# A three-layer graph kernel: heavier split rows, fewer two-sided tiles, and elementwise work moved to ScalarE and GpSimd

## The chip, the cores and the metric

One core of a Trainium2 chip. The metric is the device time of one execution in microseconds, as the median of several runs.

## The reference

The graph has N = 6250 nodes with 128 features and E = 200000 edges. The edges are sorted by destination, and destinations are drawn as 6250·u², so low-numbered nodes have hundreds to thousands of incoming edges and high-numbered ones a few dozen. The input is layer-normalised and clipped at zero. Then come three layers of the same form:

```
agg = segment_max(h[src], dst)           # per node: elementwise max over its sources' rows; 0 without edges
h   = leaky_relu(agg @ Wl + bl + h @ Wr, 0.01)
```

The widths are 128 → 256 → 256 → 128, and the output is x + h. Nearly all the work is in `segment_max`: 200000 rows of 128 or 256 floats, three times.

## The kernel before

**Tiles and planes.** Nodes are cut into 50 tiles of 127 (R = 127), sources into 25 pairs of tiles. For a tile of destinations and a source pair, TensorE multiplies the pair's rows (kept as two fp32r halves, whose sum is exact) with a one-hot matrix: each of the 128 columns picks one source row, so one product fetches one edge per destination. DVE then takes the maximum of the product in PSUM and the running result `acc` (`maxima`, line 1026). The one-hot matrix `hot` is made by ScalarE from a byte index (lines 983 and 985).

A *narrow* tile ("n") has one column set per pair: both source tiles are multiplied into the same PSUM tile, and one maximum takes it. A *middle* ("m"), *wide* ("w") or *extra* ("x") tile has one column set for each of the two source tiles, so each is multiplied and taken by itself: the same matmuls, two maxima. The nodes of the first three tiles (VT = 3) have too many edges; they are split into *virtual* rows of up to CUT_V edges in NV tiles of 128, which count as wide, with a second plane "x" each. A scan joins their parts later (`Joined`).

**Groups and steps.** The tiles form five groups: 24 narrow; the middle ones; the NV virtual with their extras; 8 wide; 4 narrow. For every group and pair there are *parts* of up to 8 tiles, which share one `hot` for each source tile. A part is cut into *steps* of 512 columns by two feature halves (layers 1 and 2) or of 1024 columns (layer 0). `parts_in` sorts the parts of a pair, and the steps follow part by part. Layer 0 has 225 steps, layers 1 and 2 have 375 each.

**Lists.** An edge that found no plane (its destination has another edge with a source in the same tile or pair) goes to a list. The lists are sorted by length, and CAPS says how many entries each block of 128 of them has. For each entry GpSimd issues one indirect DMA that gathers 128 rows from the table (`Listed.gather`, line 1064), followed by a memset of 300 elements that serves nothing but as a pause (line 1068). DVE takes the maxima of the gathered rows. There are 506 gathers in a layer. They need the whole table of the layer.

**Nodes.** When a tile's planes and lists are done, `Node` fetches its list result, merges it (DVE), multiplies by the weights (PE, line 1147 and 1149), copies the sum out of PSUM (ScalarE, 1151), applies the leaky relu (DVE, 1158 or 1162), and, for the next layer, transposes the rows and splits them into halves (`halves`; `keep_halves`, DVE, line 918).

**Making the indices.** In layer 0 the kernel still sorts the edges out. `flag_rows` finds edges that must go to lists, `pick_rows` and `rank_rows` build the lists, and `expand` finds for every pair and row the edge of that pair: each row entry holds a source number in which the tile takes the high bits, an exclusive-or with the wanted tile's number leaves a number below 128 where it fits (DVE, line 772, five pairs in five instructions), and a tree of minima finds it (778, 779). `lookups` turns that into the byte index. These pieces are *chores* that are spread over steps 0 to 150 of layer 0.

**Order.** The order of each engine's instructions is written out by hand. An agenda gives each piece a step and a rank in it (LET, TURN, MAXIMA, ROWS, REST, LINEAR, MERGE, SOONER, GATHER, FETCH). Gathers are spread evenly over a layer's steps (wide steps count 1.25), and their maxima come 6 steps later (4 at the least in layer 0). A node's `rows` comes a step after its `linear`, ahead of that step's gathers.

Of the kernel before, what the change touches and what calls it, by code (L numbers as in the profile page):

```python
# [32 lines left out]
F32 = mybir.dt.float32  # L33
# [10 lines left out]
P = 128  # L44
BIG = 2.0**127
EPS = 1e-5
SLOPE = 0.01
# [8 lines left out]
VT, NV, CUT_V = 3, 6, 96  # L56
CAPS = (
    (13, 11, 10, 9, 8, 8, 7, 7, 6, 6, 6, 6, 5, 5, 5, 4, 4, 4, 3, 3, 3, 2, 2, 1),
    (26, 22, 18, 13, 9, 5),
    (14, 11, 10, 8, 7, 7, 6, 5, 4, 4, 3),  # L60
    (33, 24, 20, 17, 15, 13, 11, 9),
    (14, 10, 8, 6),
# [5 lines left out]
HOT, HOTS = 1024, 6  # L68
# [3 lines left out]
PAUSE = 300  # L72


@with_exitstack
def kernel(ctx: ExitStack, tc: tile.TileContext, x, src, dst,
# [16 lines left out]
    PAST = NG << 8  # L93
    assert NT * P <= PAST and PAST + NT * P < LEAF
# [3 lines left out]
    NARROW = list(range(26, NT)) + list(range(22, 26))  # L98
    MIDDLE = list(range(11, 22))
# [4 lines left out]
        [("m", i) for i in range(NM)],  # L104
# [5 lines left out]
    PLANES = [units + (EXTRA[4:] + EXTRA[:4] if k == VIRT else []) for k, units in enumerate(GROUPS)]  # L110
# [165 lines left out]
    nc.vector.scalar_tensor_tensor(scol, c_i, 1.0, srci, op0=OP.add, op1=OP.add)  # L276
# [255 lines left out]
    def flag_rows(us, S):  # L532
# [6 lines left out]
        if wide:  # L539
            ri, g, o, seen = (S(i, I32, n, J) for i in (0, 1, 2, 1))  # L540
            nc.vector.tensor_copy(ri, r[:, :, :J])
            nc.vector.tensor_scalar(g, ri, 8, None, op0=OP.arith_shift_right)
            nc.vector.tensor_tensor(b, one[:, None, :].to_broadcast([P, n, J]), g, op=OP.logical_shift_left)
            nc.vector.tensor_scalar(o, ri, 24, 31, op0=OP.logical_shift_left, op1=OP.arith_shift_right)
# [33 lines left out]
    def pick_rows(k, i0, us, S):  # L578
# [12 lines left out]
        nc.vector.tensor_scalar(picked[k][:, i0 : i0 + n, :], top, -float(LEAF), 0.0, op0=OP.add, op1=OP.max)  # L591
# [174 lines left out]
    def expand(us, J, g0, s, least, S):  # L766
# [3 lines left out]
        t = S(0, I16, BATCH * n, J).rearrange("p (i u) j -> p i u j", i=BATCH)  # L770
# [12 lines left out]
    turns = itertools.cycle(("tr", "z"))  # L783
    stored = [0] * len(GROUPS)

    def lookups(us, least, s, pool, tags=("v", "v8")):

        n = len(us)
        wide = us[0][0] != "n"
        v = pool.tile([P, n, NG], BF16, tag=tags[0], name="v", bufs=1 + (tags[0] == "v"))  # L790
# [3 lines left out]
        while i < n:  # L794
# [4 lines left out]
            if us[i] in EXTRA:  # L799
                m = min(m, 4 - us[i][1] % 4)  # L800
# [85 lines left out]
    for g0 in range(0, NG, BATCH):  # L886
        expand(L0, CB, g0, 0, least, S_first)
# [27 lines left out]

    def keep_halves(layer, a, h, pr):
# [46 lines left out]
    hots, live, done_with = {}, [0], [0, 0]  # L963
# [12 lines left out]
    def one_hot(layer, k, g, c, w, odd, s):  # L976
# [4 lines left out]
        hot = work.tile([P, HOT], F32R, tag="hot", name="hot", bufs=HOTS)  # L981
# [4 lines left out]
        hots[layer, k, g, c, s] = hot  # L986
        live[0] += 1

    def products(step, s, p):
# [5 lines left out]
        hot = hots[layer, k, g, c0, s]  # L995
# [10 lines left out]
        if c * P + w == c0 * P + pw:  # L1006
            del hots[layer, k, g, c0, s]
            done_with[-1] += 1
# [20 lines left out]
    class Listed:  # L1029
# [25 lines left out]
        def gather(self, t):  # L1055
# [12 lines left out]
            nc.gpsimd.memset(gap_t, 0.0)  # L1068
# [31 lines left out]
    class Node:  # L1100
# [9 lines left out]
        def fetch(self):  # L1110
# [12 lines left out]
            if layer == 2:  # L1123
                n = min(R, N - a * R)
                self.xt = later.tile([P, D], F32, tag="xt", name="xt", bufs=4)
# [16 lines left out]
        def linear(self):  # L1142
# [163 lines left out]
    for s in range(2):  # L1306
        late_lookups(GROUPS[1], s)
# [467 lines left out]
```

## Time and profile before

| | |
|---|---|
| median of 3 runs | 3166.22 us (3161.16 to 3170.59) |
| profiled execution | 3162.05 us, span 3160.2 us |
| PE, DVE, ACT, POOL busy | 2332.1, 2717.8, 1433.9, 2430.8 us |
| gathers of the lists (POOL) | 1518, 1523.9 us, and as many pauses, 566.5 us |

The engines are PE (TensorE's matmuls), PEld (its weight loads), DVE (VectorE), ACT (ScalarE) and POOL (GpSimd). They work side by side; busy time on one hides behind another unless something waits for it. The times of stretches below count from the span's start: the setup lasts to 229 us; layer 0's steps run to 1216 us, layer 1's to 2201 us and layer 2's to about 3130 us. In layer 1 the gathers start in earnest at about 1264 us, and the first nodes are merged at about 1850 us; in layer 2 the two times are about 2260 and 2835 us.

### The profile page before, as it was taken

To read this page: it belongs to the slowest core of one execution; us is meant where nothing else is said; L and a number is where in the kernel's file an instruction comes from. 1 tells how busy PE (TensorE), PEld (TensorE's weight loads), DVE (VectorE), ACT (ScalarE), POOL (GpSimd) and SP (SyncE) were. 2 spreads that over 40 slices of the span, in tenths; PEclk is the share of its full clock that TensorE was granted. 3 is DMA by queue.
4 is the path that set the end of the run, shared out by engine and by line. 5 is a ranking of instruction groups with operands and counts; after the bars stand their busy time and mean duration, and the time that the engine had idled before them with its cause. 6 is when DMAs were issued, how large, how long until landed. Compare 5 with 4: busy or idle time off the path is not lost.

```text
span 3160.2 us, 37328 instructions
## 1 busy us (share of the span) xinstructions
PE 2332.1 (74%) x9394; PEld 1710.8 (54%) x9394; DVE 2717.8 (86%) x4441; ACT 1433.9 (45%) x2394; POOL 2430.8 (77%) x3424
## 2 busy tenths in 40 slices
PE   1024554456566778899888878889999988888997
PEld 1023333334344455677666656666676666666665
DVE  6668988987898975999999988876799999998995
ACT  5214443333544666555454434444555545443342
POOL 6666888688778883888888786763688888788882
PEclk9996766777767999999999999999999999999998
DMA  9322334266645797556454456778455554555675
GB/s 259 116 65 82 116 111 115 80 179 215 197 156 174 221 270 243 160 157 189 144 153 151 149 162 217 235 217 265 155 172 162 174 141 156 157 153 174 201 221 153
DMA packets 303458, 538.58 MB, mean 170 GB/s; under 512 B 57245, under 2 KB 165589, under 8 KB 302595
## 3 DMA queue, kind: packets, MB, share of 16 engines
q1 hardware_dynamic: 206573, 302.97, 29.7%
q0 software_dynamic: 78592, 196.07, 23.0%
q10 hardware_dynamic: 18070, 37.07, 3.1%
q8 instruction: 79, 1.29, 0.2%
q14 instruction: 144, 1.18, 0.1%
HBM read 409.84 MB, written 126.04 MB: 170 GB/s over the span
## 4 chain that ended last, share of the span: by engine, by line
DVE 19%; PE 16%; POOL 12%; DMA 6%; issue 6%; ACT 1%; SPq 0%; DVEq 0%; POOLq 0%; ACTq 0%
DVE acc L1026 13%; PE pg L1002 11%; POOL g L1064 8%; DMA g<-table,let 4%; POOL gap_t L1068 3%; DVE g L1079 2%; DVE g L1084 2%; PE z_p L1147 2%; PE z_p L1149 1%; DMA out_dram<-s 1%; DMA pair_sb<-pair 1%; ACT hot L985 0%; DMA agg_v<-best,end_i 0%; PE hT_p L908 0%; DMA xt<-in_x_dram 0%
## 5 line engine op out<-in xcount | busy, mean ns | idle before, releaser
L1002 PE MATMUL pg<-hot,pair_sb 128*128 128x512 f32 (+1 forms) x7500 | 2036.3, 421 | 414.2 <-DVE acc L1026 241.3
L1002 PEld LDWEIGHTS pg<-hot,pair_sb 128*128 128x128 f32 x7500 | 1436.1, 202 | 873.4 <-issue 285.9
L1064 POOL DMA_INDIRECT g<-table,let x1518 | 1523.9, 1004 | 492.6 <-issue 237.6
L1026 DVE TENSOR_TENSOR acc<-acc,pg 128x1024 f32<-128x1024 f32 (+4 forms) x1614 | 1663.6, 1057 | 207.1 <-PE pg L1002 164.7
L985 ACT ACTIVATE hot<-idx_sb 128x1024 fp32r<-128x1024 uint8 (+2 forms) x1050 | 909.6, 886 | 714.0 <-PE pg L1002 548.5
L1068 POOL MEMSET gap_t<- 128x300 f32 x1518 | 566.5, 373 | 0.7
L983 ACT ACTIVATE hot<-idx_sb,last_b 128x1024 fp32r<-128x1024 int8 (+1 forms) x300 | 310.3, 1034 | 37.2 <-PE pg L1002 24.9
L1118 POOL DMA_INDIRECT agg<-best,end_i x141 | 140.1, 994 | 104.1 <-PE aT_p L1134 60.5
L1151 ACT COPY s<-z_p 127x256 f32<-127x256 f32 (+1 forms) x150 | 50.4, 336 | 363.2 <-PE z_p L1149 325.8
L1079 DVE TENSOR_TENSOR g<-g 128x1024 f32<-128x1024 f32 (+6 forms) x214 | 207.8, 971 | 0.3
L1084 DVE TENSOR_TENSOR g<-g 128x256 f32<-128x256 f32 (+3 forms) x377 | 183.2, 487 | 11.2 <-issue 0.2
L1147 PE MATMUL z_p<-wr,hT_in 128*128 128x256 f32 (+1 forms) x500 | 138.7, 395 | 0.6 <-DMA hT_in<-across 0.6
L1149 PE MATMUL z_p<-wl,mz 128*128 128x256 f32 (+1 forms) x500 | 121.4, 360 | 11.9 <-DVE mz L1140 11.9
L908 PE MATMUL hT_p<-ident,h 128*128 128x128 f32 x200 | 44.3, 306 | 88.2 <-DVE h L1158 82.0
L973 DVE TENSOR_SCALAR idx_sb<-idx_sb,own_b 128x512 int32<-128x512 int32 (+3 forms) x125 | 73.4, 588 | 35.8 <-DMA idx_sb<-idx 30.6
L910 ACT COPY hT<-hT_p 128x254 f32<-128x254 f32 x100 | 37.1, 371 | 145.8 <-PE hT_p L908 129.0
L1149 PEld LDWEIGHTS z_p<-wl,mz 128*128 128x128 f32 x500 | 89.5, 204 | 25.1 <-DVE mz L1140 14.9
L652 POOL DMA_INDIRECT picks<-picked,to_i x53 | 61.5, 1161 | 48.2 <-DVE rank_f L629 23.5
L1140 DVE TENSOR_TENSOR mz<-acc,aT_p 128x256 f32<-128x256 f32 (+1 forms) x141 | 52.4, 371 | 53.3 <-PE aT_p L1134 53.3
L1147 PEld LDWEIGHTS z_p<-wr,hT_in 128*128 128x128 f32 x500 | 80.7, 203 | 31.7 <-issue 13.3
L908 PEld LDWEIGHTS hT_p<-ident,h 128*128 128x128 f32 x200 | 24.1, 149 | 120.1 <-issue 54.9
L806 ACT CAST v<-lk_p 25x1024 uint8<-25x1024 bf16 (+4 forms) x16 | 11.5, 747 | 165.7 <-PE lk_p L804 165.7
(291 smaller groups left out, 1298.0 us busy)
## 6 DMA issues: line engine op xcount, KB each, us to landing
pair_sb<-pair SPq DMA_DIRECT2D x106, 512.0 KB
idx_sb<-far SPq DMA_DIRECT2D x100, 384.0 KB
pair<-pr SPq DMA_DIRECT2D x100, 256.0 KB
g<-table,let POOLq DMA_INDIRECT x1518
pair_sb<-pair SPq DMA_DIRECT2D x85, 256.0 KB
idx_sb<-idx SPq DMA_DIRECT2D x50, 384.0 KB
far<-idx_sb ACTq DMA_DIRECT2D x50, 384.0 KB
idx_sb<-far SPq DMA_DIRECT2D x50, 352.0 KB
```

The costliest lines, as they stand in the source:

```text
L973: nc.vector.tensor_scalar(words, words, own_b.bitcast(I32)[:, 0:1], None, op0=OP.bitwise_xor)
L983: nc.scalar.activation(hot[:, :w], far_b.bitcast(I8), AF.Relu, bias=last_b, scale=-1.0)
L985: nc.scalar.activation(hot[:, :w], far_b, AF.Relu, bias=1.0, scale=-1.0)
L1002: nc.tensor.matmul(to, pr[:, s, i, kk * P : (kk + 1) * P], hot[:, o : o + bw], start=((alone or s == 0) and i == 0), stop=((alone or s == ...
L1026: nc.vector.tensor_max(to, to, of)
L1064: nc.gpsimd.indirect_dma_start(out=self.tiles[q, b][:, i, :], out_offset=None, in_=tables[self.layer], in_offset=bass.IndirectOffsetOnAxis ...
L1068: nc.gpsimd.memset(gap_t, 0.0)
L1079: nc.vector.tensor_max(base[:, : i + 1, :], base[:, : i + 1, :], g[:, : i + 1, :])
L1084: nc.vector.tensor_max(base[:, :h, :], base[:, :h, :], base[:, w - h : w, :])
L1118: nc.gpsimd.indirect_dma_start(out=self.agg[:, : self.F], out_offset=None, in_=of, in_offset=bass.IndirectOffsetOnAxis(ap=at, axis=0),)
L1147: nc.tensor.matmul(z_p, self.hT[:, i, :], wr[layer][:, i, :], start=False, stop=False)
L1149: nc.tensor.matmul(z_p, self.m[:, i, :], wl[layer][:, i, :], start=False, stop=(i == K - 1))
```

## The change

- **Distances.** Source numbers are stored with a stride of 256 instead of 128 (FAR). For wide, middle, extra and virtual rows, `expand` computes |source − 256·tile| with a ScalarE activation (Abs, the bias from a table `keys`) in place of the DVE's exclusive-or. It is issued one chore ahead of the tree that uses it, in one of four areas of scratch. Narrow rows keep the exclusive-or, and get two more DVE operations in `lookups`; `pick_rows` gets two more.
- **Relu.** ScalarE writes relu(z) and relu(−0.01·z), and GpSimd subtracts the two (`in_place`). The subtraction in `keep_halves` moves to GpSimd too. Each such operation cancels the next two pauses of the gathers (SPARE = 2; cancelled pauses are carried over when no gather follows).
- **Tiles.** NV 6 → 5 with CUT_V 96 → 104. Tiles 19 to 21 leave the middle for the narrow kind, in the same group (8 middle and 3 narrow). CAPS are new: 503 gathers a layer instead of 506.
- **Steps.** `parts_in` merges single steps of the groups, with at most two parts open at once (OPEN = 2). In layer 0 each part is one step.
- **Buffers.** Layers 1 and 2 get two more `hot` buffers (MORE = 2), and `xt` gets 8 instead of 4.

```diff
-VT, NV, CUT_V = 3, 6, 96
+VT, NV, CUT_V = 3, 5, 104
...
-    NARROW = list(range(26, NT)) + list(range(22, 26))
-    MIDDLE = list(range(11, 22))
+    NARROW = list(range(26, NT)) + list(range(22, 26)) + list(range(19, 22))
+    MIDDLE = list(range(11, 19))
...
-        [("m", i) for i in range(NM)],
+        [("m", i) for i in range(NM)] + [("n", i) for i in range(28, NN)],
...
         for i in range(BATCH):
-            nc.vector.tensor_scalar(
-                t[:, i, :, :], r[:, :, :J], ((g0 + i) << 8) | (s << 7), None, op0=OP.bitwise_xor
-            )
+            a = 2 * (g0 + i) + s
+            if wide:
+                nc.scalar.activation(t[:, i, :, :], r[:, :, :J], AF.Abs, bias=keys[:, a : a + 1], scale=1.0)
+            else:
+                nc.vector.tensor_scalar(t[:, i, :, :], r[:, :, :J], a * FAR, None, op0=OP.bitwise_xor)
...
+    def in_place(out, a, b):
+        nc.gpsimd.tensor_tensor(out, a, b, op=OP.subtract)
+        paused[0] += SPARE
+
     def keep_halves(layer, a, h, pr):
         F = widths[layer]
-        nc.vector.tensor_sub(pr[:, 1, :F], h[:, :F], pr[:, 0, :F].bitcast(F32))
+        in_place(pr[:, 1, :F], h[:, :F], pr[:, 0, :F].bitcast(F32))
...
-            nc.gpsimd.memset(gap_t, 0.0)
+            if paused[0]:
+                paused[0] -= 1
+            else:
+                nc.gpsimd.memset(gap_t, 0.0)
...
-            nc.scalar.copy(s[:R, :FO], z_p[:R, :])
+            self.h = b = h_ts[turn_h[0] % len(h_ts)]
+            turn_h[0] += 1
+            nc.scalar.activation(s[:R, :FO], z_p[:R, :], AF.Relu)
+            nc.scalar.activation(b[:R, :FO], z_p[:R, :], AF.Relu, scale=-SLOPE)
...
-                nc.vector.scalar_tensor_tensor(h[:R, :FO], s[:R, :FO], SLOPE, s[:R, :FO], op0=OP.mult, op1=OP.max)
+                in_place(h[:R, :FO], s[:R, :FO], h[:R, :FO])
...
+        open_, steps = set(), []
+        while any(rows):
+            now = sorted(r[0][:2] + (r,) for r in rows if r)
+            r = next((r for _, k, r in now if k in open_ or len(open_) < OPEN), None)
+            _, k, part, c, last = r.pop(0)
+            open_.add(k)
+            if last:
+                open_.remove(k)
+            steps.append((k, part, c))
+        return steps
```

## Rows read from the trace of the kernel before

**Rows 1.** Busy time by stretch: start:end, length, then each engine's busy us (instructions).
```profile
229.00:545.00 316.00, 160.85 (x516) 119.09 (x516) 284.38 (x655) 138.24 (x191) 259.18 (x376) 0.71 0.38 113
545.00:1216.00 671.00, 427.56 (x1421) 286.40 (x1421) 573.18 (x1166) 318.77 (x568) 529.42 (x743) 0.78 0.62 187
1264.00:1850.00 586.00, 525.43 (x2132) 391.60 (x2131) 556.60 (x596) 299.41 (x435) 510.32 (x748) 0.98 0.51 157
1850.00:2201.00 351.00, 302.29 (x1342) 227.42 (x1341) 276.86 (x355) 142.59 (x298) 225.90 (x306) 0.97 0.71 223
2260.00:2835.00 575.00, 513.85 (x2082) 379.83 (x2081) 546.29 (x587) 290.25 (x420) 496.83 (x730) 0.99 0.52 157
2835.00:3160.00 325.00, 269.61 (x1324) 206.60 (x1322) 271.79 (x378) 109.91 (x218) 225.07 (x304) 0.93 0.63 189
```

**Rows 2.** Waits of DVE, 1264 to 1850 us: total us, times, longest.
```profile
DVE acc L1026 <- PE pg L1002: 12.8, 21, 1.9
```

**Rows 3.** One line of instructions: POOL's gathers, 1264 to 1850 us.
```profile
L1064 POOL DMA_INDIRECT g<-table,let x373: 946/952/2002, 1264.4 to 1849.2; - x187
...
  issue: 55.8, 322
```

**Rows 4.** Timeline of POOL, two gathers of the lists: start us, us.
```profile
1301.16 0.95 POOL L1064 DMA_INDIRECT g<-table,let  x1 [0.17 <-issue]
...
1302.64 1.08 POOL L1064 DMA_INDIRECT g<-table,let  x1 [0.16 <-issue]
```

**Rows 5.** Chain that ended last, its part in 1264 to 1850 us, by line.
```profile
by line: DVE acc L1026 27.9%; POOL g L1064 18.7%; PE pg L1002 17.1%; issue 9.3%; DMA g<-table,let 8.8%; POOL gap_t L1068 6.7%; DVE g L1084 5.0%; DVE g L1079 3.6%; DMA idx_sb<-far 0.9%; ACT hot L985 0.7%; POOL agg_v L1188 0.3%; DVEq L1079 0.
```

**Rows 6.** Waits of POOL, 229 to 1216 us.
```profile
POOL picks L652 <- DVE rank_f L629: 23.5, 3, 19.7
...
POOL agg L1118 <- PE aT_p L1134: 19.1, 7, 7.5
```

**Rows 7.** Waits of PE, 1850 to 2201 us.
```profile
PE hT_p L908 <- DVE h L1158: 32.6, 29, 4.0
```

**Rows 8.** Groups by line and shape, DVE: xcount, busy us, mean ns, idle before.
```profile
L1026 DVE TENSOR_TENSOR acc<-acc,pg 128x1024 f32<-128x1024 f32 x1096 | 1305.9, 1216 | 149.3 <-PE pg L1002 123.5 <-ACT acc L1024 4.4 <-ACT hot L985 1.3
...
L1026 DVE TENSOR_TENSOR acc<-acc,pg 128x512 f32<-128x512 f32 x272 | 186.0, 684 | 15.8 <-PE pg L1002 5.6 <-ACT acc L1024 2.5
...
L1026 DVE TENSOR_TENSOR acc<-acc,pg 128x768 f32<-128x768 f32 x147 | 139.7, 950 | 38.0 <-PE pg L1002 35.0
...
L1158 DVE SCALAR_TENSOR_TENSOR h<-s 127x256 f32<-127x256 f32 x100 | 42.1, 421 | 8.8 <-ACT s L1151 4.9 <-DMA table<-h 3.8
...
L1026 DVE TENSOR_TENSOR acc<-acc,pg 128x384 f32<-128x384 f32 x49 | 26.9, 550 | 2.5 <-PE pg L1002 0.7
...
L1026 DVE TENSOR_TENSOR acc<-acc,pg 128x256 f32<-128x256 f32 x50 | 21.0, 420 | 1.7
...
L772 DVE TENSOR_SCALAR acc<-rows_x 128x576 int16<-128x576 int16 x50 | 19.7, 458 | 0.0
...
L1162 DVE SCALAR_TENSOR_TENSOR s<-s 127x128 f32<-127x128 f32 x50 | 14.3, 286 | 6.3 <-ACT s L1151 6.2
```

**Rows 9.** The same view, POOL's pauses and ScalarE's activations.
```profile
L1068 POOL MEMSET gap_t<- 128x300 f32 x1518 | 566.5, 373 | 0.7
...
L983 ACT ACTIVATE hot<-idx_sb,last_b 128x512 fp32r<-128x512 int8 x75 | 54.1, 721 | 12.1 <-DMA far<-idx_sb 5.0 <-DMA idx_sb<-idx 2.9 <-DMA pair_sb<-pair 2.4
...
L1151 ACT COPY s<-z_p 127x256 f32<-127x256 f32 x100 | 37.2, 372 | 191.0 <-PE z_p L1149 187.8 <-DMA pair_sb<-pair 1.9 <-DMA hT_in<-across 1.4
...
L1151 ACT COPY s<-z_p 127x128 f32<-127x128 f32 x50 | 13.2, 264 | 172.2 <-PE z_p L1149 138.0 <-DMA out_dram<-s 25.3 <-DMA xt<-in_x_dram 4.0
...
L651 POOL MEMSET gap_t<- 128x1 f32 x53 | 7.8, 148 | 0.3
```

**Rows 10.** Timeline of POOL in the setup, two gathers with no pause between.
```profile
129.52 0.94 POOL L400 DMA_INDIRECT rows_m<-cols,at_i  x1 [0.30 <-issue]
130.77 0.94 POOL L400 DMA_INDIRECT rows_m<-cols,at_i  x1 [0.30 <-issue]
```

More of the change, by code (lines that the diff above doesn't have):

```diff
@@ L44 @@
 P = 128
+FAR = 2 * P
 BIG = 2.0**127
@@ L109 @@
     EXTRA = [("x", v) for v in range(NV)]
-    PLANES = [units + (EXTRA[4:] + EXTRA[:4] if k == VIRT else []) for k, units in enumerate(GROUPS)]
+    EC = (2 * NV) % 4
+    assert 4 < NV < 8 and 2 * NV - EC == 8
+    PLANES = [units + (EXTRA[EC:] + EXTRA[:EC] if k == VIRT else []) for k, units in enumerate(GROUPS)]
     STARTS = ((0, 40, 25, 53, 60), (0, 10, 0, 19, 28), (0, 10, 0, 19, 28))
@@ L783 @@
     turns = itertools.cycle(("tr", "z"))
+    areas = itertools.cycle(range(4))
+    keys = keep.tile([P, NT], F32, name="keys")
+    nc.vector.tensor_scalar(keys, iota_f[:, :NT], -float(FAR), None, op0=OP.mult)
     stored = [0] * len(GROUPS)
@@ L789, in lookups @@
         wide = us[0][0] != "n"
+        if not wide:
+            less = pool.tile([P, n, NG], I16, tag=tags[0] + "_less", name="less")
+            nc.vector.tensor_scalar(less, least, float(FAR), float(P - FAR), op0=OP.is_ge, op1=OP.mult)
+            nc.vector.tensor_add(least, least, less)
         v = pool.tile([P, n, NG], BF16, tag=tags[0], name="v", bufs=1 + (tags[0] == "v"))
@@ L980, in one_hot @@
         far_b = t[:, at : at + w]
-        hot = work.tile([P, HOT], F32R, tag="hot", name="hot", bufs=HOTS)
+        more = layer > 0 and bool(later) and live[1] < MORE
+        if more:
+            hot = later[0].tile([P, HOT], F32R, tag="hot", name="hot_l", bufs=MORE)
+        else:
+            hot = work.tile([P, HOT], F32R, tag="hot", name="hot", bufs=HOTS)
         if s and PLANES[k][c][0] == "n":
@@ L985, in one_hot @@
             nc.scalar.activation(hot[:, :w], far_b, AF.Relu, bias=1.0, scale=-1.0)
-        hots[layer, k, g, c, s] = hot
-        live[0] += 1
+        hots[layer, k, g, c, s] = hot, int(more)
+        live[more] += 1
     def products(step, s, p):
@@ L994, in products @@
         c0, pw, _ = next(q for q in parts_of(k) if q[0] <= c < q[0] + q[1] // P)
-        hot = hots[layer, k, g, c0, s]
+        hot, more = hots[layer, k, g, c0, s]
         for b in range(0, w, 512):
@@ L1235 @@
             order.append((layer, n, g))
-            of = {}
-            for k, (c0, pw, odd), cs in parts_in(layer, ks):
+            of, begun = {}, set()
+            for k, (c0, pw, odd), c in parts_in(layer, ks):
                 first_g.setdefault((layer, k), g)
@@ L1241 @@
                     of[k] = len(blocks) - 1
-                jobs_h += [(len(steps), of[k], (layer, k, g, c0, pw, odd, s)) for s in range(2)]
-                for c in cs:
-                    steps.append((layer, k, g, c, n))
-                    ends_at[layer, k] = len(steps)
+                if (k, c0) not in begun:
+                    begun.add((k, c0))
+                    jobs_h += [(len(steps), of[k], (layer, k, g, c0, pw, odd, s)) for s in range(2)]
+                steps.append((layer, k, g, c, n))
+                ends_at[layer, k] = len(steps)
     begins.append(len(steps))
@@ L1270, in late_rows @@
         i0 = 0
-        for part in (us,):
+        for _, part in itertools.groupby(us, key=lambda u: u[0]):
+            part = list(part)
             chores.append((2.5, lambda part=part: mask_rows(part, S_acc)))
@@ L1422, in make_hots @@
     def make_hots(t, most):
-        while jobs_h and most and live[0] < HOTS and jobs_h[0][0] <= t + LOOK:
+        while jobs_h and most and jobs_h[0][0] <= t + LOOK and (
+            live[0] < HOTS or (later and jobs_h[0][2][0] > 0 and live[1] < MORE)
+        ):
             most -= 1
@@ L1447 @@
         here_now[0] = t
-        live[0] -= done_with.pop(0)
-        done_with.append(0)
+        for i, n in enumerate(done_with.pop(0)):
+            live[i] -= n
+        done_with.append([0, 0])
         if t == begins[1]:
@@ L1452 @@
             fields.close()
-            later = ctx.enter_context(tc.tile_pool(name="later", bufs=1, side="right"))
+            later.append(ctx.enter_context(tc.tile_pool(name="later", bufs=1, side="right")))
             for i in (1, 2):
-                load_layer(i, later)
+                load_layer(i, later[0])
         if t < len(steps):
```

86 lines of the change are left out of this document (49 added, 37 removed).

## The prediction

> **What bounds the kernel now.** I read the busy table by stretch first. In the long middle of layers 1 and 2 (1264 to 1850 us, 2260 to 2835 us) DVE is busy 556.6 of 586 and 546.3 of 575 us, 95% in both [rows 1], and the view of its waits finds only 12.8 us behind PE in the first of them [rows 2]. So DVE sets that pace, as it seems. But the view of POOL's gathers says that it is not alone. POOL is busy 510.3 us there [rows 1], and the 373 gathers have 322 short gaps that end on nothing, 55.8 us [rows 3]. Those gaps belong to the work: the timeline shows gathers 1302.64 − 1301.16 = 1.48 us apart, a gather, a pause of some 0.37 us and 0.16 us of issue [rows 4, 9]. 510 + 56 = 566 of 586 us: POOL has 20 us loose. The chain of waits runs through both: 27.9% DVE's maxima, 18.7% gathers, 6.7% pauses, 8.8% their transfers, 17.1% PE [rows 5]. Two engines, 97% and 95% full, are the wall there. PE is the third, at 525 us [rows 1], much of it standing behind DVE.
>
> Where nodes are made (1850 to 2201 us, 2835 to 3160 us) PE leads with 302 of 351 and 270 of 325 us [rows 1], and PE waits 32.6 us for DVE's leaky relu [rows 7]. In layer 0 the busy shares are DVE 284 of 316 us early and 573 of 671 us later, POOL 259 and 529 us [rows 1]; its 376 instructions early are 188 pairs of a DMA and a pause, its 743 later 345 such pairs and 53 fetches of nodes [rows 1]. With 0.165 us of issue for each DMA [rows 4] POOL stands at 259 + 31 = 290 of 316 us early, and at 529 + 65 = 594 of 671 us later.
>
> **The change part by part, on DVE.**
> - Distances: 200 exclusive-ors leave DVE, four kinds of 50 like the one shown, which keeps DVE busy 19.7 us (less than 50 times its mean, since neighbours overlap) [rows 8]. Two kinds, 39 us, leave the early stretch; the other two, which are shorter, leave the later one, some 37 us. What comes back: 25 exclusive-ors of narrow rows at no more than 19.7 / 50 = 0.39 us, 9 us; ten calls of `pick_rows` with two small operations, three of `lookups` with two, flags and trees for three tiles more, against smaller trees for 5 units of 104 and 8 of 48: no row has their sum, which I set at 5 us, between 0 and 15. So 14 us come back, in the later stretch.
> - Tiles 19 to 21: in layers 1 and 2 the third step of group 1 takes one 768-wide maximum where it took two: 25 × 0.950 = 24 us a layer; 25 × 0.550 = 14 us in layer 0 [rows 8].
> - Five units: the last step of the virtual group shrinks from four tiles to two: 50 maxima a layer go from 1.216 to 0.684 us, 27 us; in layer 0 from 0.684 to 0.420 us, 13 us [rows 8]. The step of mixed kinds comes out even (512 + 512 columns before, 256 + 768 after).
> - Relu and halves: 100 × 0.421 us of the relu, as many of the halves at the same 256 columns, and 50 × 0.286 us leave DVE [rows 8]: 42 us each in layers 0 and 1, 14 us in layer 2.
>
> Sum: 39 + 37 − 14 + 14 + 13 + 42 = 131 us in layer 0, 24 + 27 + 42 = 93 in layer 1, 24 + 27 + 14 = 65 in layer 2; 289 of DVE's 2717.8 us.
>
> **On ScalarE.** 200 Abs with a bias from a table, 384 to 520 columns: the same kind of activation with 512 columns takes 0.721 us [rows 9], so 144 us at the most; 150 more relus at 0.372 or 0.264 us [rows 9], 50 us. ACT is busy 138 of 316, 319 of 671 and later under 300 of 586 us [rows 1], and Abs is issued a chore ahead: I cost it at nothing. If that cover is gone, DVE's tree waits for the Abs of five pairs, 3.6 us, at 40 places.
>
> **On POOL.** A pause left out does not give back its 0.373 us [rows 9]: gathers without one are 130.77 − 129.52 = 1.25 us apart [rows 10] against 1.48, so 0.23 us. There are 250 subtractions and at most 500 cancelled pauses. No row shows a two-input operation on POOL. From below: its memset costs 0.148 us for 1 element and 0.373 for 300 [rows 9], 0.75 ns an element, so 0.148 + 256 × 0.75 ns = 0.34 us. From above: three streams (two read, one written) at that rate one after another, 0.72 us. I take the middle, 0.53 us, since neither end is nearer; for 128 columns 0.35. Set between two gathers it adds 0.53 + 0.17 − 0.30 (the issue gap it replaces [rows 10]) = 0.40 us. Layer 0: 80 in the node stretch × 0.40 = 32, against some 150 pauses × 0.23 = 35: nothing. Layer 1: 86 × 0.40 = 34 against some 118 pauses (the gathers left there) 27: 7 us more. Pauses that find no gather carry over: about 45 into layer 1's middle (10 us) and 80 into layer 2's (18 us). Nine gathers fewer: 13 us in all.
>
> The Trainium skill's GPSIMD Engine Reference (Performance versus the Vector engine, and When to use GPSIMD) speaks against the move: ordinary two-input arithmetic belongs on VectorE, since GpSimd needs about 2.6 cycles an element at 1.2 GHz. By that 256 columns are an estimated 0.55 us plus dispatch; at an estimated 0.6 us the sum would be 14 us worse over 200 operations. The trace of before has no such operation to set beside it.
>
> **Stretch by stretch**, the smaller of what DVE loses and what POOL has loose:
> - Setup, 0 to 229 us: one more pass over 1573 edges, two more operations in `pick_rows` and `lookups`. No row has their price; between 0 and 6 us, I take +3.
> - 229 to 545 us: DVE loses 39; POOL has 316 − 290 = 26 loose, some of it lost at starts: −16.
> - 545 to 1216 us: DVE loses about 92; POOL has 671 − 594 = 77 loose, of which 23.5 and 19.1 us are waits for the ranks and for PE's transposes [rows 6] that mostly stay: −35.
> - 1264 to 1850 us: DVE loses 27 + 15/25 of 24 (group 1's steps that lie before the nodes) = 41. POOL has 20 + 10 + 3 = 33: −28.
> - 1850 to 2201 us: PE's 302 us stay. The wait of 32.6 us for the relu [rows 7] now goes by ScalarE and POOL, and POOL gets 7 us more: −5, between −25 and +30.
> - 2260 to 2835 us: DVE loses 41; POOL has 575 − 497 − 52 + 18 + 3 = 47: −35.
> - 2835 to 3160 us: less relu on DVE, 8 buffers for `xt` (ACT waited 25.3 us behind the output transfers and 4.0 behind `xt` [rows 9], the first of which stay): −10.
>
> Half-size steps also save PE work: 500 matmuls of 256 columns. In the middles PE then has the more room; elsewhere no stretch that PE leads holds them, so I count nothing. Interleaved steps and more `hot` buffers even out who waits for whom; where POOL is the wall they buy nothing either.
>
> Sum: 3 − 16 − 35 − 28 − 5 − 35 − 10 = −126. The profiled execution took 3162.05 us, 4 under the median shown; 3162 − 126 = 3036.
>
> **The rivals.**
> 1. *POOL is the whole wall.* Then DVE's relief is worth nothing and only POOL's own balance counts: 250 operations cost 200 × 0.40 + 50 × 0.22 = 91, 490 pauses give 113, nine gathers 13: −35, 3127 us. For it: POOL at 97% in the middles. Against it: 77 us loose in layer 0, and PE's lead in the node stretches. 13%.
> 2. *DVE is the whole wall.* POOL's lead of six steps then covers everything and nearly all of DVE's loss is gained: 289 less a sixth for stretches led by PE, 2920 us. For it: 12.8 us of waits in 586 [rows 2]. Against it: POOL's 566 us would have to fit into 545. 12%.
> 3. *Slower: POOL held up by its subtractions.* POOL takes instructions in order; a `rows` waits for ScalarE, which waits for PE's product: 187.8 + 138.0 us over 150 copies [rows 9], 2.2 us each. Gathers and fetches stand behind it, and PE's transposes wait for its result. If the 250 operations hold POOL by 0.65 us each where nothing is loose, that is 162 us against 126: 3198 us. It decides from 0.5 us. Against it: POOL waits already in the node stretches (226 busy of 351 us [rows 1]), so a hold falls into idle time. 10%.
>
>    The Trainium skill's same page (Specifications) says that GpSimd shares its SBUF interface with VectorE where that has two SBUF inputs; DVE's list maxima are such. No run here shows it.
> 4. *It does not do what it says*: ScalarE's in-order queue makes the trees wait and eats layer 0's gain, and the carried pauses bring as much as the longer node stretch takes: within 0.3%, about 3160. 5%.
>
> **How the numbers follow.** The forecast holds 60%; its own range, from half the gains in layer 0 and the middles (3095) to all that POOL has loose (2967). Eight in ten reaches to rival 1 above and half way to rival 2 below: 2955 to 3130. A change of under 0.3% (10 us) can't be told from none. Faster: 60 + 13 + 12 = 85%, less 1 for the forecast's tail: 84%. Same 6%, slower 10%.
>
> **What would show it.** After: DVE's busy total near 2430 us; no exclusive-or on wide rows; a subtraction on POOL of 0.34 to 0.72 us; in both middles POOL's busy plus issue at 97% or more and DVE under 93%, with DVE now waiting for gathers' transfers. If DVE stays at 95% in shorter middles, rival 2 is right; if POOL idles behind ACT in the node stretches and these grow, rival 3. The forecast is wrong if the middles don't shrink by 20 to 45 us each, or layer 0 by 30 to 80.

## The result: 16.6 times slower, from a branch behind the measured work

The changed kernel takes 52666.29 us (52652.68 to 52696.58, 4 runs) against 3165.24 us (3161.16 to 3170.59, 4 runs) for the kernel before, a ratio of 16.639 [16.610, 16.667]. The forecast was 3036 us. Nothing like that stood among the rivals.

The page of the profile says where to look before any detail. Its slices are 1316 us wide; all of the kernel as it was known fits into the first three.

```profile
span 52650.9 us, 573937 instructions
...
PE 7173.1 (14%) x23735; PEld 4946.1 (9%) x23735; DVE 10914.3 (21%) x48572; ACT 1726.3 (3%) x3273; POOL 8514.8 (16%) x9619
...
POOL 7820001111111111111111111111111111111111
PEclk8965555555555555555555555555555555555555
...
L1738 POOL DMA_INDIRECT g_g<-g_table,g_i x4719 | 4447.7, 943 | 28380.0 <-PEq L1732 28233.2
...
L1656 POOL DMA_INDIRECT g_sorted<-g_pair,g_pos x1573 | 1506.2, 958 | 14476.6 <-DVEq L1632 9844.1
...
L1097 POOL DMA_INDIRECT g<-table,let x1509 | 1521.4, 1008 | 365.3 <-issue 260.3
```

The lists' gathers are there as they should be, 3 × 503 = 1509 of them. Beside them stand 4719 = 3 × 1573 gathers of line 1738, which the profile of before does not have at all, and 28.4 ms in which POOL stood idle before them. Line 1738 lies in `general_path`, a second, serial implementation for graphs that the counted lists can't hold. It is reached by this code at the end of the kernel, which the change did not touch:

```python
nc.tensor.matmul(falls_p[:, :2], ones, bad, start=True, stop=True)
nc.tensor.matmul(falls_p[:, 2:], ones, over, start=True, stop=True)
...
general = nc.values_load(falls_i[0:1, 0:1], min_val=0, max_val=1)
with tc.If(general > 0):
    general_path(...)
```

`over` has a column for each list; `rank_rows` writes into it for how many lengths more rows are that long, or longer, than the list has room for. The longest length that a list may have is `reach = min(CAPS[k][0] + 4 * PACK[k], DEEP[k] - 1)`; beyond it there is room for none, so one longer row is enough. For the third list (group 1) the change raised the first cap from 14 to 16, but DEEP stayed 24: min(16 + 12, 23) = 23.

The timeline at that point (start us, us, engine, line, operation) shows the test and what follows it.

```profile
3045.92 0.37 PE L1550 MATMUL falls_p<-over,ones 128*128 128x9 f32 x2
...
3046.82 0.15 DVE L1555 CAST falls_i<-falls_s 128x1 int32<-128x1 f32 x1
3048.90 0.83 SPq L1711 DMA_DIRECT2D g_xt<-in_x_dram  x2
3049.19 1.37 DVE L1575 MEMSET g_dsti<- 128x1573 int32 x1 [2.22 <-DMA out_dram<-s]
```

The same product (line 1495 there) ran at 3149.92 us before. So the changed kernel came to its end 104.0 us *earlier*, and then ran another 49.6 ms. Deep inside that stretch the timeline repeats one pattern:

```profile
30006.17 0.94 POOL L1738 DMA_INDIRECT g_g<-g_table,g_i  x1 [6.34 <-PEq L1732]
30009.05 0.48 DVE L1742 SCALAR_TENSOR_TENSOR g_state<-g_state,g_m,g_g 128x256 f32<-128x256 f32 x1 [3.30 <-DMA g_g<-g_table,g_i]
30012.80 0.15 DVE L1734 COPY g_i<-g_srci 128x1 int32 x1 [3.27 <-PEq L1732]
...
30013.49 0.95 POOL L1738 DMA_INDIRECT g_g<-g_table,g_i  x1 [6.38 <-PEq L1732]
```

One gather of 128 rows each 7.3 us, one after another: gather, its transfer, a maximum, the next round of a loop. By the row of line 1738 above, these gathers and the idle time before them are 4.4 + 28.4 = 32.8 of the 49.6 ms. The loops that sort the edges before that (line 1656) take most of the rest, 1.5 + 14.5 = 16.0 ms by the same count.

### The profile page after: what moved, and what is told of

Read it like the earlier page. It is cut to its first block, busy times and chain, and to the rows that moved or that the text cites. A ratio compares the mean times of both kernels' runs of the same rounds, so it can differ in the third digit from the quotient of the medians.

```text
span 52650.9 us, 573937 instructions
## 1 busy us (share of the span) xinstructions
PE 7173.1 (14%) x23735; PEld 4946.1 (9%) x23735; DVE 10914.3 (21%) x48572; ACT 1726.3 (3%) x3273; POOL 8514.8 (16%) x9619
## 5 line engine op out<-in xcount | busy, mean ns | idle before, releaser
L1738 POOL DMA_INDIRECT g_g<-g_table,g_i x4719 | 4447.7, 943 | 28380.0 <-PEq L1732 28233.2
L1742 DVE SCALAR_TENSOR_TENSOR g_state<-g_state,g_m,g_g 128x256 f32<-128x256 f32 (+1 forms) x4719 | 2076.1, 440 | 14970.1 <-DMA g_g<-g_table,g_i 14970.1
L1656 POOL DMA_INDIRECT g_sorted<-g_pair,g_pos x1573 | 1506.2, 958 | 14476.6 <-DVEq L1632 9844.1
L1622 PE MATMUL g_count<-g_oa_t,g_ob_t 128*128 128x49 f32 x6292 | 2038.0, 424 | 3723.3 <-DVE g_ob_t L1617 3623.5
L1622 PEld LDWEIGHTS g_count<-g_oa_t,g_ob_t 128*128 128x128 f32 x6292 | 1574.9, 311 | 4394.6 <-issue 3832.1
L1035 PE MATMUL pg<-hot,pair_sb 128*128 128x512 f32 (+2 forms) x5980 | 1618.7, 418 | 366.7 <-DVE acc L1059 155.2
L1059 DVE TENSOR_TENSOR acc<-acc,pg 128x1024 f32<-128x1024 f32 (+5 forms) x1539 | 1537.8, 1025 | 300.3 <-PE pg L1035 258.1
L1644 PE MATMUL g_at_p<-g_nxt,g_obT 128*128 128x49 f32 x3146 | 1043.9, 432 | 603.0 <-DVE g_obT L1642 603.0
L1644 PEld LDWEIGHTS g_at_p<-g_nxt,g_obT 128*128 128x128 f32 x3146 | 789.8, 312 | 1065.5 <-DVE g_obT L1642 1065.5
L1617 DVE TENSOR_SCALAR g_ob_t<-iota_f,g_ab_t 128x128 f32<-128x128 f32 x3146 | 878.4, 279 | 0.0
```

The costliest lines, as they stand in the source:

```text
L1035: nc.tensor.matmul(to, pr[:, s, i, kk * P : (kk + 1) * P], hot[:, o : o + bw], start=((alone or s == 0) and i == 0), stop=((alone or s == ...
L1059: nc.vector.tensor_max(to, to, of)
L1617: nc.vector.tensor_scalar(ob, iota_f, c[:, 1:2], None, op0=OP.is_equal)
L1622: nc.tensor.matmul(p, ob, oa, start=True, stop=True)
L1644: nc.tensor.matmul(at_p, obT, nxt, start=True, stop=True)
L1656: nc.gpsimd.indirect_dma_start(out=sorted_, out_offset=bass.IndirectOffsetOnAxis(ap=pos[:, :1], axis=0), in_=pair, in_offset=None,)
```

## The profile after, stretch by stretch

The part before 3047 us can be compared with before. Equal work is marked off by the maxima's products (line 1035, 1002 before): 500 and 1000 of them in layer 0; in layers 1 and 2 the stretch of 2000 behind the first 200, and the last 800. First the kernel before (start:end, length, busy us and instructions of PE, PEld, DVE, ACT, POOL, granted clock, DMA share, GB/s), in the order layer 0 early and late, layer 1 middle and nodes, layer 2 middle and nodes.

```profile
229.00:563.00 334.00, 167.51 (x537) 124.46 (x538) 301.83 (x681) 143.52 (x198) 275.39 (x396) 0.71 0.37 110
563.00:1216.00 653.00, 420.90 (x1402) 281.03 (x1400) 555.73 (x1140) 313.49 (x561) 513.21 (x723) 0.79 0.63 191
1284.00:1835.00 551.00, 493.80 (x1997) 367.65 (x1998) 524.82 (x566) 276.84 (x403) 479.40 (x704) 0.98 0.51 159
1836.00:2201.00 365.00, 314.56 (x1394) 236.73 (x1393) 289.95 (x366) 150.34 (x309) 237.97 (x323) 0.97 0.70 219
2270.00:2820.00 550.00, 494.06 (x1999) 365.18 (x2000) 522.14 (x559) 276.11 (x400) 474.82 (x701) 0.99 0.52 159
2820.00:3150.00 330.00, 282.60 (x1380) 216.55 (x1378) 285.66 (x388) 118.16 (x229) 238.07 (x322) 0.94 0.64 191
```

Then the changed kernel, the same work, and its last row the general path.

```profile
230.00:547.00 317.00, 170.74 (x530) 123.01 (x531) 259.87 (x552) 204.19 (x297) 263.35 (x383) 0.71 0.38 115
547.00:1185.00 638.00, 405.31 (x1398) 278.95 (x1396) 483.01 (x982) 366.55 (x700) 523.82 (x678) 0.78 0.63 186
1253.00:1782.00 529.00, 476.94 (x2004) 364.21 (x2002) 488.19 (x543) 270.19 (x402) 455.99 (x641) 0.98 0.51 157
1782.00:2131.00 349.00, 311.99 (x1376) 238.36 (x1375) 253.62 (x274) 160.02 (x346) 261.54 (x291) 0.95 0.73 229
2202.00:2726.00 524.00, 474.14 (x2002) 361.48 (x2002) 487.13 (x543) 269.27 (x402) 450.24 (x628) 0.98 0.52 159
2726.00:3047.00 321.00, 273.60 (x1374) 211.66 (x1374) 263.69 (x334) 124.51 (x275) 240.26 (x303) 0.96 0.66 199
3047.00:52650.00 49603.00, 4905.89 (x14364) 3249.92 (x14364) 8461.77 (x44642) 173.11 (x539) 6098.44 (x6445) 0.50 0.07 22
```

| stretch | forecast | in this trace |
|---|---|---|
| setup | +3 | +1 |
| layer 0 early, late | −16, −35 | −17, −15 |
| layer 1 middle, nodes | −28, −5 | −22, −16 |
| layer 2 middle, nodes | −35, −10 | −26, −9 |
| sum | −126 | −104 |

The forecast's stretches begin and end up to 20 us away from these. The first 200 products of layers 1 and 2 stand in no row: they took 68 and 69 us before and take 68 and 71 now.

Now the groups of instructions that answer to [rows 8, 9] and to the bounds put on GpSimd's subtraction: POOL's and ScalarE's rows of 0 to 3047 us (count, then busy us, mean ns, then the idle time before them).

```profile
L942 POOL TENSOR_TENSOR pr<-h,pr 128x256 fp32r<-128x256 f32 x100 | 79.4, 794 | 45.3 <-ACT pr L936 38.8 <-PE z_p L1181 5.8 <-DMA hT_in<-across 0.2
L942 POOL TENSOR_TENSOR h<-s,h 127x256 f32<-127x256 f32 x100 | 76.9, 769 | 44.1 <-ACT h L1190 42.4 <-DMA pair<-pr 0.5
L942 POOL TENSOR_TENSOR s<-s,h 127x128 f32<-127x128 f32 x50 | 23.7, 475 | 35.7 <-ACT h L1190 32.0 <-DMA out_dram<-s 2.0 <-ACT let L1086 1.1
...
L1104 POOL MEMSET gap_t<- 128x300 f32 x1033 | 385.8, 373 | 0.5
```
```profile
L784 ACT ACTIVATE acc<-rows_w,keys 128x520 int16<-128x520 int16 x50 | 31.7, 713 | 10.2 <-DVE acc L625 10.2
```

The subtraction costs 0.77 to 0.79 us, above the upper bound of 0.72 that was put on it, and 1509 − 1033 = 476 pauses were cancelled, where 490 were reckoned with. In the two middles no subtraction runs. There the waits of POOL's gathers (1253 to 1782 us) answer to [rows 3], and DVE's waits to [rows 2]:

```profile
L1097 POOL DMA_INDIRECT g<-table,let x345: 941/952/1935, 1252.4 to 1781.0; - x173
...
  issue: 54.2, 291
```
```profile
DVE acc L1059 <- PE pg L1035: 28.2, 36, 2.4
DVE acc L1059 <- ACT acc L1057: 0.7, 1, 0.7
```

456 + 54 = 510 of 529 us on POOL, 96%; DVE 488 of 529, 92%. In layer 2's middle the two are 450 + 56 = 506 and 487 of 524 us, 97% and 93%. The prediction asked for 97% or more and under 93%, so these two signs are met or missed by about a point. Its third sign is missing: DVE was to wait for the gathers' transfers, but the second fence is the view's whole answer for this stretch, and no transfer stands in it, nor in the answer for layer 2's middle (24.2 us behind PE, 0.8 behind ScalarE). DVE's waits behind PE, 12.8 us in [rows 2] over 586 us, are 28.2 us over 529. Over the whole part up to 3047 us DVE is busy 2452.6 us (forecast about 2430).

## The experiments

They ran on four chips (experiments 1 to 3, 4 to 7, 8 to 11, and 12), on which the kernel before takes 3200 to 3231 us; so what is compared is the ratio to runs of before on the same chip. Such a ratio can differ by 0.3% from the quotient of the two medians. The differing base is not explained: no trace of before was taken there.

**1. The third list gets room.** The smallest edit that lets the suspected test pass.

```diff
-DEEP = (24, 40, 24, 48, 24)
+DEEP = (24, 40, 32, 48, 24)
```

> The changed kernel with one number more changed: the third entry of DEEP is 32 instead of 24, so the mixed list (8 middle and 3 narrow tiles) may be up to 28 entries deep instead of 23. Theory A (one row of that list has 26 edges left over, more than the 23 that the list holds, the kernel's own test sees it, and the general path then runs after the fast one): the general path is gone, the span ends where the fast path ended in the trace after, about 3047 us, time 3045 to 3060 us. Theory B (another bound is broken: more virtual rows than 5 x 128, or source numbers that no longer fit the arithmetic): the branch is still taken and the time stays at 52660 us.

3149.25 us (3137.6 to 3153.17) against 3208.74, ratio 0.9805 [0.9781, 0.983]. The general path is gone, though the time is 90 to 100 us above what was expected from the trace of after. The longest row of the third list has more than 23 edges and, since reach is now min(28, 31), no more than 28. Counted from the inputs by the kernel's rule it is one row of 26; before the change the longest had 19. Two things make it so long. A narrow tile keeps one edge for a pair of source tiles, and it offers only the first 32 edges of a row to its planes (CB), where a middle tile offers 48 (CUT_B); the rest go to the list. By the same count this row of 42 edges would leave 23 with 48 slots, and the test would have passed.

**2. The third list's test alone is silenced.** DEEP stays 24; the edges that one row has beyond the list are left out of one node's maximum.

```diff
         nc.vector.reduce_sum(over[:, k : k + 1], sums[:, 0, : V - 1], axis=AX.X)
+        if k == 2:
+            nc.vector.memset(over[:, k : k + 1], 0.0)
```

> The changed kernel with the sum of the third list's test set to zero; it leaves out the edges that this list can't hold (two or three edges of one node). Theory A: about 3050 us, since no other test fails. Theory B: 52660 us. If this is fast and the deeper list is not, the fault lies in how the test counts and not in the list's depth.

3146.2 us, one run, the same as experiment 1. No other test fires, and the larger DEEP costs nothing that shows.

**3. Tiles 19 to 21 back in the middle kind**, with that list's CAPS of before and DEEP 24.

```diff
...
-    NARROW = list(range(26, NT)) + list(range(22, 26)) + list(range(19, 22))
-    MIDDLE = list(range(11, 19))
+    NARROW = list(range(26, NT)) + list(range(22, 26))
+    MIDDLE = list(range(11, 22))
...
```

> The changed kernel with tiles 19 to 21 back among the middle tiles, with the list lengths of before for that group; DEEP stays at 24. Theory A: it is the move of the three tiles to one edge per source pair that leaves 26 edges of one row over (19 at most before), so here the general path does not run; DVE gets back 24 us a layer in layers 1 and 2 and 14 in layer 0, less what the three narrow tiles had added in layer 0, and GpSimd loses 13 gathers a layer (58 us). If GpSimd is the wall, it is the faster of the two fast versions, 3020 to 3050 us; if DVE is, the slower, 3070 to 3110 us. Theory B: 52660 us.

3174.78 us (3170.13 to 3192.58), ratio 0.9892 [0.9873, 0.9912]: no general path, so these tiles are what made the list too long. It also prices them, together with the 13 gathers a layer that the shorter list saves: 0.9% against experiment 1 on the same chip. The middle of layer 1, experiment 1 and then this:

```profile
1311.00:1838.00 527.00, 471.27 (x2000) 360.25 (x2000) 487.86 (x544) 270.02 (x402) 447.73 (x633) 0.98 0.52 155
```
```profile
1293.00:1856.00 563.00, 487.49 (x2002) 370.77 (x2000) 502.20 (x560) 269.95 (x400) 436.44 (x625) 0.96 0.49 146
```

36 us more for 14 us more of DVE's work, with DVE at 89% and POOL less busy. So DVE's added work cost more here than its own time, with no engine full: POOL now waits 70.9 us in that stretch for the ScalarE instruction that hands out the gathers' indices, against 13.1 in experiment 1.

The following runs all have DEEP 32 in the third place; the diffs show what else differs. Experiment 1 was run again beside the first three of them.

**4. Experiment 1 again.**

> The deeper list once more, as the base that the other three of this call are set against. 3149 us against 3209 for the kernel before in the first call (ratio 0.98); the trace of the changed kernel ended its fast path at 3047 us against a span of 3160, a ratio of 0.964. If the machine makes the difference (its transfers at the start and at the layers' seams were slower in the first call), the ratio here lies anywhere in 0.963 to 0.982, and the middle stretches take 525 to 530 us as in both traces.

3165.77 us (3157.33 to 3179.91) against 3230.7, ratio 0.9791 [0.9764, 0.9819]. Two chips agree on 2%.

**5. No pauses at all.**

```diff
-            if paused[0]:
-                paused[0] -= 1
-            else:
-                nc.gpsimd.memset(gap_t, 0.0)
```

> The deeper list without any pause behind a gather: 1033 memsets fewer, 0.23 us each, 237 us off GpSimd. Theory W (GpSimd is the wall of the middles, as the prediction has it): the two middle stretches fall from 527 to about 490 us each, until DVE's 488 us fill them, and layer 0 by 20 us; 3149 to 3050 on the machine of the first call, ratio to r5 0.965 to 0.98. Theory D (DVE and PE, handing three PSUM tiles to and fro, are the wall, and GpSimd's gathers keep their lead): within 15 us of r5, ratio 0.995 to 1.0; slower, if gathers packed closer disturb the other transfers.

3388.63 us (3380.86 to 3400.93), ratio 1.0492 [1.0456, 1.0529], 7% slower than experiment 4. Of what was expected only the last words, "slower, if gathers packed closer disturb the other transfers", point that way, and they give no size. 1033 instructions and 385 us of POOL's work are gone, and everything is later. The row of the middle (1400 to 1800 us) of experiment 4, then of this one:

```profile
1400.00:1800.00 400.00, 360.31 (x1527) 275.80 (x1526) 372.93 (x418) 204.89 (x310) 354.52 (x516) 0.98 0.53 157
```
```profile
1400.00:1800.00 400.00, 340.41 (x1377) 261.61 (x1376) 329.58 (x371) 184.78 (x274) 233.09 (x232) 0.92 0.48 143
```

DVE's instructions are no longer than they were (329.58 / 371 = 0.89 us, 372.93 / 418 = 0.89 us); there are fewer of them in 400 us. The waits of the whole run (us, times, longest) show which grew; experiment 4 first.

```profile
PEld pg L1035 <- issue: 310.1, 197, 19.0
...
PE pg L1035 <- issue: 139.1, 69, 18.6
...
POOL g L1097 <- ACT let L1086: 95.9, 35, 18.8
...
DVE acc L1059 <- remote: 48.7, 12, 10.7
```
```profile
PEld pg L1035 <- issue: 460.3, 291, 21.1
...
POOL g L1097 <- ACT let L1086: 336.3, 92, 26.1
...
PE pg L1035 <- issue: 243.9, 132, 18.0
...
DVE acc L1059 <- remote: 176.1, 50, 16.7
```

On PE and DVE, which have no gathers, most of the growth is in waits that end on nothing which the profile shows ("issue", "remote"). POOL then stands behind the others. TensorE's granted clock is lower too, 0.92 against 0.98 in the rows of 1400 to 1800 us; whether as a cause or a result is not shown. What delays the engines when gathers follow one another without a pause stays open. Nor does it happen everywhere: in the trace of after the first 200 products of layers 1 and 2 run beside 22 and 24 gathers without one pause, and take no longer than before (68 and 71 us against 68 and 69). On the chip of experiment 4 the same kernel with the deeper list takes 84 and 91 us there.

**6. Relu and halves back on DVE**, ScalarE copying as before.

```diff
-        in_place(pr[:, 1, :F], h[:, :F], pr[:, 0, :F].bitcast(F32))
+        nc.vector.tensor_sub(pr[:, 1, :F], h[:, :F], pr[:, 0, :F].bitcast(F32))
...
-            nc.scalar.activation(s[:R, :FO], z_p[:R, :], AF.Relu)
-            nc.scalar.activation(b[:R, :FO], z_p[:R, :], AF.Relu, scale=-SLOPE)
+            nc.scalar.copy(s[:R, :FO], z_p[:R, :])
...
-                in_place(h[:R, :FO], s[:R, :FO], h[:R, :FO])
+                nc.vector.scalar_tensor_tensor(h[:R, :FO], s[:R, :FO], SLOPE, s[:R, :FO], op0=OP.mult, op1=OP.max)
...
```

> The deeper list with the leaky relu and the subtraction of the halves back on DVE as in the kernel before; all pauses stay. DVE gets back 98 us, GpSimd loses 250 operations of 0.78 and 0.46 us and gets 485 pauses back. Theory W: within 10 us of r5 in the middles, since only the carried-over pauses lie there, and in all 0 to 25 us slower. Theory D: the node stretches and layer 0 lose the 42 us a layer where DVE is late: 30 to 60 us slower. A rival to both (GpSimd's subtraction holds up the gathers, as the prediction's third rival has it): faster than r5 by 10 us or more.

3163.26 us (3153.27 to 3166.78), ratio 0.9796 [0.9773, 0.9819], the same as experiment 4. By equal work the two node stretches are longer (394 and 358 us against 354 and 346), the first 200 products of layers 1 and 2 shorter (63 and 66 against 84 and 91): with no subtraction no pause is cancelled, and none is missing there. On this chip the move is worth something where nodes are made and is given back at the start of the next layer.

**7. Steps part by part, as before.** `parts_in` returns its steps in the old order.

```diff
...
+            at = sorted(((i + 0.5) / len(ps), k, part) for k, ps in mine.items() for i, part in enumerate(ps))
+            return [(k, part, c) for _, k, part in at for c in parts[k, part]]
```

> The deeper list with the steps in the old order, part by part (two wide steps or two narrow ones in a row). Theory W: the same as r5 within 10 us, since the order of steps changes no engine's sum. Theory D: in layers 1 and 2 DVE runs dry in pairs of narrow steps and PE stands in pairs of wide ones, so the middles lose most of what they gained, 15 to 30 us each, 30 to 60 us in all.

3159.72 us (3137.76 to 3165.3), ratio 0.9762 [0.9717, 0.9806]. The merged order is worth nothing that can be measured.

**8. No pause cancelled.**

```diff
-SPARE = 2
+SPARE = 0
```

> The deeper list with SPARE = 0: GpSimd keeps the relu and the subtraction, but no pause is cancelled, 476 memsets more than r5, some 110 us of GpSimd time. Theory G (packed gathers hold the other engines up, as the run without pauses showed; cancelled pauses do the same on a small scale at the layers' starts): faster than the base's ratio of 0.980 to the kernel before, 0.960 to 0.972, the first 25 steps of layers 1 and 2 at 65 us instead of 84 to 91. Theory W (GpSimd's own time counts): slower than the base, 0.985 to 1.0. If neither counts, 0.976 to 0.984.

3146.76 us (3140.9 to 3161.43) against 3200.34, ratio 0.9806 [0.9776, 0.9835]: the same again. The starts of the layers take 68 and 70 us as in the trace of before (68, 69), against 84 and 91 in experiment 4. In layer 1 the node stretch gives most of that back (368 against 354); in layer 2 it does not (342 against 346), and the profiled execution as a whole is some 19 us shorter, which the ratio does not bear out.

**9. Distances back on DVE.**

```diff
-            if wide:
-                nc.scalar.activation(t[:, i, :, :], r[:, :, :J], AF.Abs, bias=keys[:, a : a + 1], scale=1.0)
-            else:
+            if True:
                 nc.vector.tensor_scalar(t[:, i, :, :], r[:, :, :J], a * FAR, None, op0=OP.bitwise_xor)
```

> The deeper list with the exclusive-ors of the wide rows back on DVE (200 instructions, 76 us of DVE time in steps 0 to 125 of layer 0; the Abs leave ScalarE). If DVE bounds layer 0: ratio 0.998 to 1.005, layer 0 longer by 50 to 70 us. By the prediction, which let GpSimd bound the early stretch: 20 to 45 us longer, ratio 0.986 to 0.994. If layer 0's gain comes from neither: 0.978 to 0.983.

3168.57 us (3158.25 to 3175.5), ratio 0.9875 [0.9839, 0.991]; by the ratios 0.7 to 0.8% over experiments 1, 4 and 8. Early layer 0 takes 327 us instead of 315, the late part 660 instead of 661 (experiment 8).

**10. Six units again.**

```diff
-VT, NV, CUT_V = 3, 5, 104
+VT, NV, CUT_V = 3, 6, 96
...
-    (29, 23, 18, 13, 9),
+    (26, 22, 18, 13, 9, 5),
...
-    EC = (2 * NV) % 4
+    EC = 4
```

> The deeper list with six virtual units of 96 edges as before (93 entries in their list instead of 92). DVE gets back 27 us a layer in layers 1 and 2 and 13 in layer 0, PE 500 matmuls at double width (up to 59 us). If DVE and PE bound the middles: slower than the base by 40 to 65 us, ratio 0.993 to 1.0, most of it between steps 25 and 275 of layers 1 and 2. If GpSimd bounds them: within 10 us of the base, 0.977 to 0.984.

3176.59 us (3169.35 to 3198.92), ratio 0.9937 [0.9892, 0.9981]. By the ratios five units are worth 1.3 to 1.5%, by the medians against experiment 8 on the same chip 0.9%; the middles are 540 and 538 us with six, 527 to 534 with five (experiments 1, 4 and 8).

**11. Longer pauses**, all of them kept.

```diff
-PAUSE = 300
-SPARE = 2
+PAUSE = 450
+SPARE = 0
```

> As r9, with pauses of 450 elements instead of 300, 0.11 us more for each of 1509 gathers. Theory G alone (more room helps further): faster than r9 by up to 1%. With GpSimd nearly full in the middles (443 us busy and some 55 of issue in 527), 373 x 0.11 = 41 us more there make it the wall: slower than r9 by 30 to 80 us, ratio 0.975 to 0.995. I hold the second the likelier.

3314.59 us (3301.15 to 3317.02), ratio 1.033 [1.0292, 1.0369], 168 us over experiment 8, at least twice the 30 to 80 us that were expected. The pause of experiment 8, then of this run:

```profile
L1104 POOL MEMSET gap_t<- 128x300 f32 x1509 | 559.5, 371 | 0.8
```
```profile
L1104 POOL MEMSET gap_t<- 128x450 f32 x1509 | 751.4, 498 | 0.7
```

0.127 us more, 1509 times, are 192 us; 168 of them come through to the end. The middles, with some 345 pauses, should grow by 44 us if POOL were the whole wall; they grow from 534 to 570 and 571, by 36. In the first of them DVE now waits 28.9 us for the gathers' transfers, against 4.5 in experiment 8.

**12. Shorter pauses**, cancelled as in the change.

```diff
-PAUSE = 300
+PAUSE = 220
```

> The deeper list with pauses of 220 elements instead of 300 (SPARE = 2 as in r5), 0.06 us less for each of the 1033 pauses that remain, 62 us off GpSimd. If GpSimd is full in the middles and packing hurts only when gathers come back to back: faster than the base's ratio of 0.980, 0.970 to 0.978, each middle 5 to 15 us shorter. If every shortening of the pause costs the other engines, as the run without pauses suggests: slower, 0.99 to 1.03, layer 0 and the middles longer.

3166.71 us (3151.72 to 3173.19) against 3207.69, ratio 0.9858 [0.9821, 0.9895]: between the two expectations, not faster than 300 elements, rather slower (middles 547 and 540 us against 527 to 534). So longer pauses cost nearly their full time, and shorter ones bring nothing: in the first middle POOL then waits 51.6 us for the ScalarE instruction that hands out its indices, against 12.6 in experiment 4.

No run forced the kernel before into its general path; that path's 49.6 ms are read from the one trace of after.

## Why the prediction was wrong

**The step that failed: a part of the change was read only for its work.** "Tiles 19 to 21 leave the middle for the narrow kind" was priced as one maximum saved a pair, and CAPS as "nine gathers fewer". That a narrow tile keeps one edge for a pair of source tiles where a middle one keeps two, and takes only 32 slots of a row instead of 48, that its rows therefore leave more edges to the list, and that the list's depth is a constant beside CAPS, entered no term. Nor did the rival "It does not do what it says" think of it: it spoke of lost overlap. A test that the kernel makes of its own input was in the code, with a branch of unknown price behind it, and was treated as if it could not change. Experiments 1 to 3 show it: room in the list, silence of its test, and the tiles put back each remove the branch, and nothing else is needed.

**The rest of the sum, measured without the branch.**
- *Sizes by stretch.* −104 in the trace of after against −126. The two middles gave 22 and 26 of a forecast 28 and 35, late layer 0 15 of 35, layer 1's node stretch 16 where 5 were forecast. Early layer 0's −17 for −16 is partly luck: GpSimd was to use up some 16 of the 26 us that it had loose there, yet has 317 − 263 − 29 = 25 us left.
- *GpSimd's subtraction: mis-sized.* 0.53 us forecast, 0.77 to 0.79 measured, beyond the bound; 0.35 and 0.475 for 128 columns. The Trainium skill's GPSIMD Engine Reference (Performance versus the Vector engine) has the two engines at a measured ratio of 1.96 for such an addition over 2048 columns; with DVE's 0.421 us [rows 8] that would be an estimated 0.83 us, nearer to this trace than the estimate of 0.55 us plus dispatch from its cycles an element.
- *Rival 3's mechanism (POOL held up by its subtractions): not seen.* In late layer 0 POOL is fuller than before, 524 + 61 = 585 of 638 us against 513 + 55 = 568 of 653. But PE does not wait longer for the rows that it transposes. First before (563 to 1216 us), then after (547 to 1185 us):

```profile
PE hT_p L908 <- DVE h L1158: 48.8, 17, 6.8
```
```profile
POOL g L1097 <- issue: 60.8, 285, 0.9
...
PE hT_p L931 <- POOL h L942: 35.2, 15, 6.8
...
PE hT_p L931 <- POOL pr L942: 9.3, 3, 3.4
```

  In layer 1's node stretch the wait that was 32.6 us [rows 7] is 4.7 us.
- *POOL's and DVE's shared wall.* Borne out in part. Experiment 11 denies rival 2 (DVE the whole wall, with POOL's lead covering everything): of 192 us of pauses 168 came through, so POOL had next to no room. Experiments 3, 9 and 10 deny rival 1 (POOL the whole wall), since DVE's work still costs time (experiment 10 adds PE's too); in experiment 3 POOL even had fewer gathers. But in the trace of after DVE waits for no transfer in the middles, so that POOL held DVE up there is not shown.
- *"A pause left out gives 0.23 us": wrong.* Experiment 5 leaves 1033 out and loses 223 us, experiment 8 puts 476 back and loses nothing.
- *ScalarE's distances at nothing: too little.* An Abs of 520 columns takes 0.713 us, as its nearest row said [rows 9], and DVE's trees wait for them 24.2 us in all. But PE now waits longer in layer 0 for the one-hot matrices that ScalarE also makes: 69.9 us early and 32.8 later, where it was 29.7 and 13.8. The largest rows of the early stretch, before and after:

```profile
PE pg L1002 <- ACT hot L983: 27.5, 3, 14.4
```
```profile
PE pg L1035 <- ACT hot L1016: 66.9, 17, 15.4
```

  With the distances back on DVE (experiment 9) these waits are 45.6 and 8.4 us, against 51.7 and 20.5 in experiment 8, so the distances have a part in them. How much of late layer 0's missing 20 us that makes is not shown.
- *Interleaved steps bring nothing: right* (experiment 7).
- *A slip in the range.* The 2955 of "eight in ten" is not half way to rival 2's 2920: from 3036 that is 2978, from 2967 it is 2944.

**How much the change is worth with the list mended** is less settled than the table. By the stretches of the one trace it is 104 of 3150 us, 3.3%, and that trace is of the fastest of four executions, 1.4 to 44 us shorter than the others. By experiments 1 and 4 it is 2.0% and 2.1%, half of the forecast's 126 of 3162 us, 4.0%. In experiment 1 the middles are those of after (527, 528 us), but setup, late layer 0, the starts of layers and the node stretches are longer, 96 us to the end. Part of it, 14 and 22 us at the starts, goes when every gather has its pause (experiment 8). Without a trace of before from those chips it stays open how much of that the kernel before has there too. The version that beats both kernels is that of experiments 1 and 4; no variant of it measured clearly faster.

## What to carry to other kernels

Where a kernel tests its own input and branches, list every constant that the test compares with (here DEEP, PACK and CAPS) and what feeds it (here the kind of a tile and CB), and recompute its margin for each edit that changes what is counted; a branch of unknown price is a rival with a chance of its own. When a time is wrong by a factor, look for lines in the table of groups that the profile of before does not have, before any engine's share. An instruction that serves only as a pause is measured, not priced: its removal can cost more than its time.

## What the runs showed of the hardware

- Gathers issued with no pause between them slowed PE and DVE, on the chip of experiments 4 to 7, by waits that end on nothing in the profile: ratio 1.049, where pauses of 0.37 us give 0.979 with a third of them left out and 0.981 with all. Pauses of 0.50 us give 1.033, of 220 elements 0.986. In the trace of after, 22 and 24 gathers without a pause at the starts of two layers cost nothing that shows. The cause was not found.
- GpSimd's subtraction of two 256-column tiles takes 0.77 to 0.79 us and of two 128-column tiles 0.475 us, so an estimated 0.17 us and 2.4 ns a column, where its memset takes 0.75 ns a column [rows 9].
- In the general path, where PE ran at long intervals, its granted clock was 0.50 of 2.4 GHz, the lower level, against 0.91 up to 3047 us.
